# Gate, up and the experts' first weights as seven block products in place of eight, in a gated MLP with a mixture of experts

## The chip, the core and the metric

The kernel runs on one NeuronCore of a Trainium2 chip. The metric is device time in microseconds (us): the median of several executions. One execution was also recorded by the hardware profiler. The engines are TensorE (PE, with its weight loads as PEld), VectorE (DVE), ScalarE (ACT), GpSimd (POOL), and SyncE (SP), which here only issues transfers. Each engine takes its instructions in one fixed order, which the compiler has chosen from the program's text and the dependences.

## What is computed

1024 tokens of 512 features are normalised (layer norm). From the result `xn` two things are made and multiplied, and the input is added:

```python
s = silu(xn @ w_gate.T)                   # 1024 x 1376
k = 1376 // 2
# per token: the k entries of smallest |s| become 0
s = s.at[rows, top_k(-abs(s), k)].set(0.0)
s = (s * (xn @ w_up.T)) @ w_down.T        # 1024 x 512

scores = softmax(xn @ router_w + router_b) + router_bias   # 16 experts in 4 groups
# the 2 best groups, and in them the 2 best experts of each token
y = sum over experts e: gate[e] * ((silu(xn @ w1[e] + b1[e]) * (xn @ w2[e] + b2[e])) @ w3[e] + b3[e])
z = the same form with the shared weights (inner size 256, as two experts of 128)
out = x + s * silu(y + z)
```

Everything is fp32. w1 and w2 of an expert are 512 x 128, w3 is 128 x 512.

## The kernel before

`quick_path` does all the work in the case at hand; a second path, `general_path`, would run after it only if a flag said that the quick search had failed, or that more than two routed experts were used. The tokens are eight tiles of 128. An fp32 matmul takes two passes of TensorE.

**Inputs.** SP loads tile 0 of x, the first 512 columns of the gate weights, tiles 1 to 3, the rest of the gate weights, and then the router's weights, which stand as 16 more columns behind the gate's 1376 (`GW` = 1392). `stats` (L565) and `normalise` (L585) make mean and deviation on DVE in a chain of small operations, subtract and scale; PE transposes the tile into `xnT`, 4 chunks of 128 features by 1024 tokens, and ACT copies it out of PSUM.

**Gate.** `gate(t, k)` (L601 to L617) multiplies a tile by one of the three column ranges `COLS` (512, 512, 352; the last with the router's 16 columns: 368). Four chunks accumulate in one of eight PSUM banks, ACT applies silu, `S[t]` takes the result. `absolute` (L619) makes magnitudes `A[t]` and their sum on ACT, into buffers with the tag `row`.

**Search.** `Search` (L632) finds for each token the threshold below which exactly half of its magnitudes lie. It begins from the mean; each of four `step`s counts the entries under the candidate and corrects it. A count is one pass over 1376 entries, on DVE (L648) or on ACT (L653); the first search, tiles 0 to 3, puts two of four counts on DVE, the second, tiles 4 to 7, none. `last` (L668) does three passes per tile on DVE (count, keep those below, eight greatest), `thresholds` picks the exact value in eight small operations, and `mask` (L706) zeroes the small entries.

**Experts.** `choose` finds each token's experts; `fetch` makes row numbers from it and gathers the weights of the two experts in use by indirect transfers on POOL's queue. `expert` (L856) multiplies 512 tokens at a time by w1 and w2, silu on ACT, product on DVE.

**Up and down.** `up(t)` (L842) has the form of `gate`; DVE multiplies its result into `S[t]` (L853). `finish(t)` (L875) does the second expert products (L881), sums them with the gates on DVE, applies silu, transposes `S[t]` on PE (L905, ACT copies to `sT`), multiplies by `w_down` (L921, 11 chunks), and multiplies and adds on DVE and POOL (L924, L926). Then SP stores the tile.

The program's order is: gate of tiles 0 to 3, the first search beside gate of tiles 4 to 7, shared experts, last of the first search, up of tiles 0 to 3, the second search, up of tiles 4 to 7, routed experts, and the eight `finish`. `wd_sb` uses the gate weights' memory and is loaded when the gate is done.

Of the kernel before, what the change touches and what calls it, by code (L numbers as in the profile page):

```python
# [19 lines left out]
P = 128  # L20
H = 512
# [22 lines left out]
ROW_BUFS = 5  # L44
SLOTS = 2
GW = I + E

# [434 lines left out]
def quick_path(  # L482
# [16 lines left out]
    NT = N_TOK // P  # L499

# [6 lines left out]
    dram = ctx.enter_context(tc.tile_pool(name="dram", bufs=1, space=DRAM))  # L507
# [6 lines left out]
    def load_x(t, again=""):  # L514
        xt = work.tile([P, H], F32, tag="x", name=f"x{again}{t}", bufs=4)
        nc.sync.dma_start(xt, x[ts(t, P), :])
        return xt

    wg_sb = big.tile([P, IC * H], F32, tag="wgd", name="wg_sb")[:, : HC * GW].rearrange(
        "p (c n) -> p c n", c=HC  # L520
    )
    wg_v = wg.rearrange("(c p) n -> p c n", p=P)

    X = {0: load_x(0)}
    lo, n = COLS[0]
    for c in range(HC):
        nc.sync.dma_start(wg_sb[:, c, :n], wg[ts(c, P), :n])  # L527
    for t in range(1, 4):
        X[t] = load_x(t)
    for lo, n in COLS[1:]:  # L530
        nc.sync.dma_start(wg_sb[:, :, lo : lo + n], wg_v[:, :, lo : lo + n])
    nc.sync.dma_start(wg_sb[:, :, I:], rw)
# [10 lines left out]
    b3s_sb = const.tile([P, H], F32, tag="b3s", name="b3s_sb")  # L543
    nc.gpsimd.dma_start(b3s_sb, b3[E].partition_broadcast(P))
# [16 lines left out]
    xnT = big.tile([P, HC, N_TOK], F32, tag="xnT", name="xnT")  # L561
    mv = const.tile([P, NT, 2], F32, tag="mv", name="mv")
    rstd = const.tile([P, NT], F32, tag="rstd", name="rstd")

    def stats(t0, n):  # L565
        for t in range(t0, t0 + n):
            st = small.tile([P, 6], F32, tag="st", name=f"st{t}")
            nc.vector.bn_stats(st, X[t])  # L568
            nc.vector.bn_aggr(mv[:, t, :], st)


        r = rstd[:, t0 : t0 + n]
        ve = small.tile([P, n], F32, tag="ve", name=f"ve{t0}")
        nc.vector.tensor_single_scalar(ve, mv[:, t0 : t0 + n, 1], EPS, ALU.add)
# [3 lines left out]
        q = small.tile([P, n], F32, tag="q", name=f"q{t0}")  # L578
# [6 lines left out]
    def normalise(t0, n):  # L585
        for t in range(t0, t0 + n):
            xn = work.tile([P, H], F32, tag="xn", name=f"xn{t}")
            nc.vector.tensor_scalar(
                xn, X[t], mv[:, t, 0:1], rstd[:, t : t + 1], ALU.subtract, ALU.mult
            )  # L590
            pt = psum(f"pt{t}")
            for c in range(HC):
                nc.tensor.transpose(pt[:, ts(c, P)], xn[:, ts(c, P)], ident)
            nc.scalar.copy(xnT[:, :, ts(t, P)], pt.rearrange("p (c n) -> p c n", c=HC))  # L594
# [6 lines left out]
    def gate(t, k):  # L601
        lo, n = COLS[k]
        w = n + E if k == 2 else n
        if k == 0:
            S[t] = rows.tile([P, I], F32, tag=f"s{t}", name=f"s{t}")
        pz = psum(f"pz{t}_{lo}")
        for c in range(HC):
            nc.tensor.matmul(  # L608
                pz[:, :w],
                xnT[:, c, ts(t, P)],  # L610
                wg_sb[:, c, lo : lo + w],
                start=(c == 0),
                stop=(c == HC - 1),
            )
        nc.scalar.activation(S[t][:, lo : lo + n], pz[:, :n], AF.Silu)  # L615
        if k == 2:
            nc.vector.tensor_tensor(lg[:, t, :], pz[:, n : n + E], rb_sb, ALU.add)  # L617

    def absolute(t):  # L619
        A[t] = row(f"a{t}")[:, :I]  # L620
        nc.scalar.activation(A[t], S[t], AF.Abs, accum_out=asum[:, t : t + 1])  # L621
# [10 lines left out]
    class Search:  # L632
        def __init__(self, t0, n, on_dve):
            self.t0, self.n, self.on_dve = t0, n, on_dve
# [6 lines left out]
        def step(self, k):  # L641
            t0, n = self.t0, self.n
            d = small.tile([P, n], F32, tag="d", name=f"d{t0}_{k}")
            for i in range(n):
                c, cnt = self.c[:, i : i + 1], d[:, i : i + 1]
                if i < self.on_dve:
                    junk = work.tile([P, I], BF16, tag="junk_d", name=f"jd{t0}_{k}_{i}", bufs=1)
                    nc.vector.tensor_scalar(  # L648
                        junk, A[t0 + i], c, None, ALU.is_lt, ALU.add, accum_out=cnt
                    )  # L650
                else:
                    junk = work.tile([P, I], BF16, tag="junk_a", name=f"ja{t0}_{k}_{i}", bufs=1)
                    nc.scalar.activation(  # L653
                        junk, A[t0 + i], AF.Sign, bias=c, scale=-1.0, accum_out=cnt
# [13 lines left out]
        def last(self, i0, i1):  # L668
            t0, n = self.t0, self.n
            if i0 == 0:  # L670
                self.cnt = small.tile([P, n], F32, tag="cnt", name=f"cnt{t0}")
                self.v = small.tile([P, n, 8], F32, tag="v", name=f"v{t0}")
            for i in range(i0, i1):
                w = rows.tile([P, I], F32, tag="w", name=f"w{t0 + i}")
                nc.vector.tensor_scalar(
                    w, A[t0 + i], self.c[:, i : i + 1], None, ALU.is_lt, ALU.add,
                    accum_out=self.cnt[:, i : i + 1],
                )
                nc.vector.scalar_tensor_tensor(  # L679
                    w, A[t0 + i], self.c[:, i : i + 1], A[t0 + i], ALU.is_lt, ALU.mult  # L680
                )
                nc.vector.max(self.v[:, i, :], w)

        def thresholds(self):
# [19 lines left out]
            nc.vector.tensor_scalar(bad[:, t0 : t0 + n], over, -1.0, 1.0, ALU.mult, ALU.add)  # L704
# [385 lines left out]
```

## Time and profile before

| What | Value |
|---|---|
| Median of three runs | 346.39 us (345.88 to 347.0) |
| The profiled execution's own time | 346.43 us |
| Its span, first to last instruction | 344.6 us |
| PE busy | 327.0 us, 95% of the span |
| PEld busy | 161.2 us, 47% |
| DVE busy | 158.7 us, 46% |
| ACT busy | 90.7 us, 26% |
| POOL busy | 22.3 us, 6% |
| Mean granted clock of PE | 0.993 |
| Moved by DMA | 18.99 MB |

Busy times are the union of an engine's instructions; an engine that is busy for a small share of the span may still be full in one stage. The profile gives instructions in groups: the line of the program, the engine, the operation, what is written from what is read, partitions x elements, how many, their busy time and the mean ns of one, and the engine's idle time just before them with what ended it. The chain of waits goes back from the last instruction, at each step to what released it. Its costliest lines are L921 (22% of the span), L846 (21%) and L608 (21%).

### The profile page before, as it was taken

The page shows a single profiled execution, that of the slowest core. Times are in us where ns is not written, and L with a number is a line of the kernel's source. Part 1 is how long each engine was busy: PE and PEld are TensorE (multiplying, and loading weights), DVE is VectorE, ACT ScalarE, POOL GpSimd, SP SyncE. Part 2 cuts the span into 40 slices and gives each one's busy share as a digit, 9 for nine tenths or more (in the row PEclk, how much of TensorE's full clock was granted, in tenths as well). Part 3 has the DMA queues.
Part 4 walks back from the last instruction along what each step waited for, and adds up shares of the span by engine and source line. Part 5 has one row for each costly group of instructions (what it writes and reads, how often), then busy time and mean ns, then how long its engine had stood idle before and what let it go on. Part 6 is the DMA issues. An engine that isn't in the chain of part 4 may idle for free.

```text
span 344.6 us, 2574 instructions
## 1 busy us (share of the span) xinstructions
PE 327.0 (95%) x898; PEld 161.2 (47%) x898; DVE 158.7 (46%) x353; ACT 90.7 (26%) x149; POOL 22.3 (6%) x30
## 2 busy tenths in 40 slices
PE   1899999999999999999999999999999999999991
PEld 0344465444444444445454444454454544544480
DVE  4752005999978323987983300123150431504300
ACT  1322169861169787000000010020120201202010
POOL 4000000000000000460000000001010010110100
PEclk9999999999999999999999999999999999999997
DMA  6989002000090000160000000000010110000000
GB/s 193 324 307 355 2 0 61 0 1 2 2 320 6 0 0 2 39 187 18 0 0 2 0 0 1 0 2 34 27 61 0 63 50 11 30 0 30 33 19 22
DMA packets 10165, 18.99 MB, mean 55 GB/s; under 512 B 1360, under 2 KB 2688, under 8 KB 10144
## 3 DMA queue, kind: packets, MB, share of 16 engines
q1 hardware_dynamic: 9328, 16.35, 13.6%
q0 software_dynamic: 816, 2.39, 2.6%
q8 instruction: 9, 0.15, 0.2%
q14 instruction: 12, 0.10, 0.1%
HBM read 16.65 MB, written 2.10 MB: 54 GB/s over the span
## 4 chain that ended last, share of the span: by engine, by line
PE 92%; DMA 2%; DVE 2%; ACT 1%; SPq 1%; issue 0%
PE po L921 22%; PE pu L846 21%; PE pz L608 21%; PE pys L881 4%; PE pbr L863 4%; PE par L863 4%; PE pbs L863 4%; PE pas L863 4%; PE pyr L881 4%; PE ps L905 3%; DMA x<-in_x_dram 2%; SPq L527 0%; ACT xnT L594 0%; ACT a L621 0%; DVE st L568 0%; ACT s L615 0%
## 5 line engine op out<-in xcount | busy, mean ns | idle before, releaser
L608 PE MATMUL pz<-wg_sb,xnT 128*128 128x512 f32 (+1 forms) x192 | 78.7, 571 | 1.7 <-ACT xnT L594 1.6
L921 PE MATMUL po<-wd_sb,sT 128*128 128x512 f32 (+3 forms) x198 | 77.7, 549 | 0.0
L846 PE MATMUL pu<-wu_sb,xnT 128*128 128x512 f32 (+1 forms) x192 | 74.2, 548 | 0.0
L608 PEld LDWEIGHTS pz<-wg_sb,xnT 128*128 128x128 f32 x192 | 37.2, 196 | 41.4 <-issue 31.3
L846 PEld LDWEIGHTS pu<-wu_sb,xnT 128*128 128x128 f32 x192 | 36.4, 190 | 37.4 <-issue 29.7
L921 PEld LDWEIGHTS po<-wd_sb,sT 128*128 128x128 f32 (+1 forms) x198 | 37.0, 190 | 36.1 <-issue 33.5
L924 DVE TENSOR_TENSOR g<-po,g 128x512 f32<-128x512 f32 (+1 forms) x9 | 5.7, 632 | 70.5 <-PE po L921 70.5
L653 ACT ACTIVATE ja<-a,c 128x1376 bf16<-128x1376 f32 x24 | 34.6, 1440 | 6.3 <-DVE c L666 5.9
L907 ACT COPY sT<-ps 128x512 f32<-128x512 f32 (+1 forms) x24 | 11.5, 516 | 92.9 <-PE ps L905 92.9
L615 ACT ACTIVATE s<-pz 128x512 f32<-128x512 f32 (+1 forms) x24 | 13.1, 547 | 44.1 <-PE pz L608 44.1
L870 ACT ACTIVATE hr<-par,bs 128x512 f32<-128x512 f32 x4 | 2.8, 688 | 80.9 <-PE par L863 80.9
L853 DVE TENSOR_TENSOR s<-s,pu 128x512 f32<-128x512 f32 (+1 forms) x24 | 14.6, 626 | 10.9 <-PE pu L846 10.9
L926 POOL TENSOR_TENSOR g<-g,xr 128x512 f32<-128x512 f32 x7 | 8.8, 1263 | 162.3 <-DVE g L924 162.3
L881 PE MATMUL pys<-w3shared,hs 128*128 128x512 f32 x32 | 15.1, 595 | 0.0
L881 PE MATMUL pyr<-w3slot,hr 128*128 128x512 f32 x32 | 15.0, 592 | 0.0
L863 PE MATMUL pas<-xnT,w12shared 128*128 128x512 f32 x32 | 14.4, 592 | 0.0
L863 PE MATMUL pbs<-xnT,w12shared 128*128 128x512 f32 x32 | 14.4, 592 | 0.0
L863 PE MATMUL par<-xnT,w12slot 128*128 128x512 f32 x32 | 14.4, 592 | 0.0
L863 PE MATMUL pbr<-xnT,w12slot 128*128 128x512 f32 x32 | 14.4, 592 | 0.0
L871 DVE SCALAR_TENSOR_TENSOR hr<-pbr,bs,hr 128x512 f32<-128x512 f32 x4 | 3.0, 750 | 23.1 <-PE pbr L863 23.1
L648 DVE TENSOR_SCALAR_CACHE_REDUCE jd<-a,c 128x1376 bf16<-128x1376 f32 x8 | 13.2, 1646 | 0.2
L679 DVE SCALAR_TENSOR_TENSOR w<-a,c 128x1376 f32<-128x1376 f32 x8 | 13.2, 1648 | 0.1
(124 smaller groups left out, 235.9 us busy)
## 6 DMA issues: line engine op xcount, KB each, us to landing
wd_sb<-in_wd_dram SPq DMA_DIRECT2D x1, 2560.0 KB, 10.5
x<-in_x_dram SPq DMA_DIRECT2D x8, 256.0 KB, 5.7
wu_sb<-in_wu_dram SPq DMA_DIRECT2D x2, 1024.0 KB, 9.7
xr<-in_x_dram SPq DMA_DIRECT2D x8, 256.0 KB, 2.8
out_dram<-g SPq DMA_DIRECT2D x7, 256.0 KB, 2.0
wg_sb<-in_wg_dram SPq DMA_DIRECT2D x4, 256.0 KB, 5.8
wg_sb<-in_wg_dram SPq DMA_DIRECT2D x1, 1024.0 KB, 9.8
w12shared<-in_wexp_dram SPq DMA_DIRECT2D x2, 512.0 KB, 5.5
```

What stands on the lines that cost most here:

```text
L608: nc.tensor.matmul(pz[:, :w], xnT[:, c, ts(t, P)], wg_sb[:, c, lo : lo + w], start=(c == 0), stop=(c == HC - 1),)
L615: nc.scalar.activation(S[t][:, lo : lo + n], pz[:, :n], AF.Silu)
L648: nc.vector.tensor_scalar(junk, A[t0 + i], c, None, ALU.is_lt, ALU.add, accum_out=cnt)
L653: nc.scalar.activation(junk, A[t0 + i], AF.Sign, bias=c, scale=-1.0, accum_out=cnt)
L679: nc.vector.scalar_tensor_tensor(w, A[t0 + i], self.c[:, i : i + 1], A[t0 + i], ALU.is_lt, ALU.mult)
L846: nc.tensor.matmul(pu[:, :n], xnT[:, c, ts(t, P)], wu_sb[:, c, lo : lo + n], start=(c == 0), stop=(c == HC - 1),)
L853: nc.vector.tensor_mul(S[t][:, lo : lo + n], S[t][:, lo : lo + n], pu[:, :n])
L863: nc.tensor.matmul(pk, w[0][:, k * H + c * P : k * H + (c + 1) * P], xnT[:, c, cols], start=(c == 0), stop=(c == HC - 1),)
L881: nc.tensor.matmul(py, h[:, ts(t, P)], w, start=(i == 0), stop=(i == len(which) - 1))
L905: nc.tensor.transpose(pt[:w, ts(c - c0, P)], s[:, c * P : c * P + w], ident)
L907: nc.scalar.copy(sT[:, c0 : c0 + full, :], pt[:, : full * P].rearrange("p (c n) -> p c n", c=full),)
L921: nc.tensor.matmul(po, sT[:w, c, :], wd_sb[:w, c, cols], start=(c == 0), stop=(c == IC - 1))
```

## The change

A product of two matrices cut into 2 x 2 blocks takes eight block products; Strassen's form (here with Winograd's sums) takes seven, and additions of blocks ahead of them and behind. In the changed kernel:

- Two tiles, j and j + 4, make a pair: the first is the upper, the second the lower block row. The 512 features are halved into the block columns. `xs` holds seven blocks: A11, A12, A21, A22 and the sums S1, S2, S4; S3 replaces A21. `sums(j)` makes them with four DVE operations.
- The weights' columns are halved too (gate 2 x 696 with the router's columns, up 2 x 688, an expert's w1 and w2). `weight_sums` makes T1, T2, T4, and replaces B12 by T3, with four operations, on DVE (`V`) or POOL (`G`) as listed.
- `Unit` is a set of seven products, in four PSUM banks X, Y, W, Z, for a pair and a quarter of the columns (344 or 348 wide), or for an expert and 512 tokens. Part `a` makes X and Y, `b` makes W and Z, `c` accumulates three more products on X, W and Z. U = X + Y and V = W + Z are formed in between by an ACT copy and a DVE addition each. `Line.push` interleaves a unit's `a`, the previous unit's `c`, and the unit's `b`.
- Of the gate's four results only the first is silu'd out of PSUM; the other three are sums with U or V that are written to `S` first, and `absolute` applies silu to them in memory. In up the sums go to `tmp`, and POOL multiplies three of the four quarters into `S`.
- There are four searches of two tiles each, with one count on DVE and one on ACT. They are handed to `Line.push` as work to be placed behind a unit's `c`.
- Memory: the gate weights' space later holds the hidden values and the second expert's weights; `wu` and then `wd` share one space, so that `wd` is loaded after up. `row` has four buffers in place of five.
- The order is: gate of the four pairs, the shared experts, the first routed expert, up of pair 0, the second routed expert, up of pairs 1 to 3, and then the eight `finish`, with the expert products of three tiles ahead.

```diff
+    def sums(j):
+        def blk(b):
+            return xs[:, b, :, ts(j, P)]
+        nc.vector.tensor_add(blk(S1), blk(A21), blk(A22))
+        nc.vector.tensor_sub(blk(S3), blk(A11), blk(A21))
+        nc.vector.tensor_sub(blk(S2), blk(S1), blk(A11))
+        nc.vector.tensor_sub(blk(S4), blk(A12), blk(S2))
+    def weight_sums(eng, b11, b21, b12, b22, t1, t2, t4):
+        first = eng[0].tensor_tensor(t1, b12, b11, ALU.subtract)
+        eng[1].tensor_tensor(b12, b22, b12, ALU.subtract)
+        eng[2].tensor_tensor(t2, b22, t1, ALU.subtract)
+        eng[3].tensor_tensor(t4, b21, t2, ALU.subtract)
+        return first
...
+        def a(self):
+            self.X, self.Y = self.acc("x"), self.acc("y")
+            self.mm(self.X, A11, "b11", True, True)
+            self.mm(self.Y, S2, "t2", True, True)
+            self.U = work.tile([P, HALF], F32, tag="U", name=f"U{self.name}")[:, : self.n]
+            nc.scalar.copy(self.U, self.X)
+            self.summed = nc.vector.tensor_tensor(self.U, self.U, self.Y, ALU.add)
+        def b(self):
+            self.W, self.Z = self.acc("w"), self.acc("z")
+            self.mm(self.W, S1, "t1", True, True)
+            self.mm(self.Z, S3, "b12", True, True)
+            self.V = work.tile([P, HALF], F32, tag="V", name=f"V{self.name}")[:, : self.n]
+            nc.scalar.copy(self.V, self.W)
+            nc.vector.tensor_tensor(self.V, self.V, self.Z, ALU.add)
+        def c(self):
+            self.mm(self.X, A12, "b21", False, True)
+            self.mm(self.W, S4, "b22", False, True)
+            self.mm(self.Z, A22, "t4", False, True)
+            self.sink(self)
...
+    def gate_unit(d, j, q):
...
+        def sink(u):
+            l, r = slice(q * n, (q + 1) * n), slice(half + q * n, half + (q + 1) * n)
+            nc.scalar.activation(top[:, l], u.X, AF.Silu)
+            nc.vector.tensor_tensor(top[:, r], u.W, u.U, ALU.add)
+            nc.vector.tensor_tensor(bot[:, l], u.Z, u.U, ALU.add)
+            add = nc.gpsimd if j < NP - 1 else nc.vector
+            add.tensor_tensor(bot[:, r], u.U, u.V, ALU.add)
...
+    def up_unit(d, j, q):
...
+        def sink(u):
+            nc.vector.tensor_mul(top[:, l], top[:, l], u.X)
+            for s, acc, which in ((top[:, r], u.W, "w"), (bot[:, l], u.Z, "z")):
+                m = tmp(u, which)
+                nc.vector.tensor_tensor(m, acc, u.U, ALU.add)
+                nc.gpsimd.tensor_tensor(s, s, m, ALU.mult)
+            nc.gpsimd.tensor_tensor(u.U, u.U, u.V, ALU.add)
+            nc.gpsimd.tensor_tensor(bot[:, r], bot[:, r], u.U, ALU.mult)
...
+    def expert_unit(name, w, b1, b2, h):
...
+        def sink(u):
+            nc.scalar.activation(ht, u.X, AF.Silu, bias=b1)
+            m = tmp(u, "z")
+            nc.vector.tensor_tensor(m, u.Z, u.U, ALU.add)
+            nc.scalar.activation(hb, m, AF.Silu, bias=b1)
+            m = tmp(u, "w")
+            nc.vector.tensor_tensor(m, u.W, u.U, ALU.add)
+            nc.vector.scalar_tensor_tensor(ht, m, b2, ht, ALU.add, ALU.mult)
+            nc.vector.tensor_tensor(u.U, u.U, u.V, ALU.add)
+            nc.vector.scalar_tensor_tensor(hb, u.U, b2, hb, ALU.add, ALU.mult)
...
+        g = work.tile([P, H], F32, tag=("U", "V", "tmp")[t % 3], name=f"g{t}")
...
+    for j in range(NP):
...
+        if j == 0:
+            sum_quarter(dg, 0, GQ, [V, V, V, G])
+        sums(j)
+        if j == 0:
+            sum_quarter(dg, GQ, GQ, [V, G, V, G])
...
+        def begin(j=j):
+            if j:
+                search[j - 1].step(2)
+                search[j - 1].step(3)
+                select(j - 1)
+            absolute(j)
+            search[j] = Search(j)
+        line.push(gate_unit(dg, j, 0), steps(j - 1, (0, 1)) if j else None)
+        line.push(gate_unit(dg, j, 1), begin)
...
+    line.push(shared(0, w12_first))
+    nc.sync.dma_start(w12_second[:, : 2 * H], wexp[E + 1, :, : 2 * H])
+    chosen = choose()
+    line.push(shared(1, w12_second), steps(NP - 1, (0, 1, 2, 3)))
+    routed, mix, fetch_weights = fetch(*chosen, [w12_third, w12_second], slot_w3)
+    du = blocks(wu_sb, I // 2, "u")
+    for q in range(2):
+        sum_quarter(du, q * UQ, UQ, [G, G, G, G])
+    fetch_weights(0)
+    line.push(routed_unit(0), lambda: select(NP - 1))
+    fetch_weights(1)
+    for j in range(NP):
+        for q in range(2):
+            line.push(up_unit(du, j, q))
+            if (j, q) == (0, 1):
+                line.push(routed_unit(1))
+    line.flush()
...
+    wd_sb = big.tile([P, IC * H], F32, tag="wB", name="wd_sb").rearrange("p (c n) -> p c n", c=IC)
...
+    ahead = 3
+    gt = {t: experts_out(t, ex, mix) for t in range(ahead)}
     for t in range(NT):
-        if t < 4:
-            qb.mask(t)
-        finish(t, ex, mix)
+        finish(t, gt.pop(t))
+        if t + ahead < NT:
+            gt[t + ahead] = experts_out(t + ahead, ex, mix)
```

`experts_out(t)` is the first half of what was `finish(t)`: the second expert products, their sum with the gates, and silu. `select(j)` is `last`, `thresholds` and the two masks of pair j.

## The prediction

> **What bounds it now.** I read the chain of waits first, then the same chain in order of time, then busy times by stage, then rows by shape. The chain is almost all TensorE:
>
> ```profile
> PE 92%; DMA 2%; DVE 2%; ACT 1%; SPq 1%; issue 0%
> ```
>
> In order of time (start, length, what) from 22.56 us to 337.15 there is no gap that matters in it; three pieces price a matmul pass:
>
> ```profile
> 55.82 37.63 PE pz L608 x96
> ...
> 93.45 3.43 PE pas L863 x8
> ...
> 120.92 9.23 PE pu L846 x24
> ```
>
> Eight passes of 512 columns take 3.43, one 0.429. A tile of up (16 passes of 512, 8 of 352) takes 9.23, so a 352-wide pass takes (9.23 - 6.86)/8 = 0.296. A tile of gate takes 37.63/4 = 9.41. An fp32 matmul is two passes.
>
> Busy times by stage (stretch, length, then PE, PEld, DVE, ACT, POOL):
>
> ```profile
> 0.00:22.56 22.56, 12.92 (x32) 6.01 (x32) 13.04 (x63) 5.46 (x8) 3.58 (x15) 1.00 0.80 260
> 22.56:55.80 33.24, 32.72 (x96) 16.89 (x96) 6.44 (x28) 12.15 (x21) 0.00 (x0) 1.00 0.37 132
> 55.80:93.45 37.65, 37.63 (x97) 18.51 (x98) 35.03 (x60) 20.30 (x32) 0.00 (x0) 1.00 0.04 13
> 93.45:120.90 27.45, 27.45 (x66) 12.14 (x65) 18.10 (x55) 21.09 (x29) 0.00 (x0) 1.00 0.30 103
> 120.90:195.00 74.10, 74.10 (x196) 36.71 (x195) 47.85 (x95) 12.87 (x19) 9.84 (x8) 1.00 0.10 29
> 195.00:222.50 27.50, 27.50 (x67) 11.90 (x65) 4.42 (x5) 2.75 (x4) 0.00 (x0) 1.00 0.00 0
> 222.50:337.20 114.70, 114.64 (x352) 59.01 (x350) 33.03 (x48) 16.12 (x40) 8.84 (x7) 1.00 0.08 27
> ```
>
> The reader is to see the DVE column: to 222.5 it sums to 124.9, over half of the time, and in the search it is 93% busy already. The last stage, which the change hardly touches, is where DVE is free.
>
> **PE: what is removed.** Each unit of a pair of tiles is 7 products x 2 chunks x 2 passes = 28 passes. At 348 columns (0.292, in proportion to 352) gate is 8 units x 28 x 0.292 = 65.4 in place of 8 x 9.41 = 75.3; up, at 344 (0.289), 64.7 in place of 73.8; the experts 4 x 28 x 0.429 = 48.0 in place of 16 x 3.43 = 54.9. Removed: 9.9 + 9.1 + 6.9 = 25.9 us. The weight load stays hidden: its rows are 190 ns, under a pass of 289.
>
> **Start.** At 22.56 PE had done two gate groups and four tiles' transposes, 6.9 + 2.1 = 9.0 us, as if it had begun at 13.6 without a gap. After, the second product needs tile 4, both sums and the weight sums. Tile 4 is the fourth transfer, behind 0.97 MB (tile 1 was behind 1.31 MB and came at 9.9): about 8. Then a serial chain as tile 0 shows it, 3.24 to 9.5, gives 14.3, less the sums; four sums in series, 4 x 0.46, overlap in part: 15.5. By then 2.2 us of PE work is done and, the first gate group having taken 6.61 where 3.43 is usual, some 2 are lost to a slow start: as if from 15.3, 1.7 later. Bounds -1 and +6 (tile 4 as late as tile 1, loads of short rows).
>
> PE alone: 346.43 - 25.9 + 1.7 = **322.2**.
>
> **DVE: what is added.** Rows by shape:
>
> ```profile
> L679 DVE SCALAR_TENSOR_TENSOR w<-a,c 128x1376 f32<-128x1376 f32 x8 | 13.2, 1648 | 0.1
> L648 DVE TENSOR_SCALAR_CACHE_REDUCE jd<-a,c 128x1376 bf16<-128x1376 f32 x8 | 13.2, 1646 | 0.2
> L853 DVE TENSOR_TENSOR s<-s,pu 128x512 f32<-128x512 f32 x16 | 10.7, 682 | 7.5 <-PE pu L846 7.5
> L926 POOL TENSOR_TENSOR g<-g,xr 128x512 f32<-128x512 f32 x7 | 8.8, 1263 | 162.3 <-DVE g L924 162.3
> L853 DVE TENSOR_TENSOR s<-s,pu 128x352 f32<-128x352 f32 x8 | 4.1, 514 | 3.4 <-PE pu L846 3.4
> L924 DVE TENSOR_TENSOR g<-po,g 128x256 f32<-128x256 f32 x2 | 0.8, 424 | 9.3 <-PE po L921 9.3
> ```
>
> - `sums`: 16 x 0.424 = 6.8. `weight_sums` on DVE: 5 of 696 elements (0.69 + 184 x 1.05 ns = 0.885) = 4.4, and 16 of 256 for the experts = 6.8.
> - Gate units, which cost DVE nothing before: 34 x 0.51 = 17.4. Expert units: 5 more each of 512, 20 x 0.69 = 13.8. Up: 40 x 0.51 less 14.8 now = 5.6.
> - Search: one count of two on DVE in place of two of eight, 8 more x 1.73 (with the accumulator's read) = 13.8. ACT loses as many. Steps' small operations, 96 for 44, 52 x 0.165 = 8.6; starts and `thresholds` for four searches in place of two, 3.6.
> - `stats`: one more chain of 15 x 0.155 = 2.3.
>
> Sum 83.1: DVE needs 124.9 + 83.1 = **208 us** before the down stage can run freely, PE only 183. Bounds: 202 operations are added; of independent operations the next begins before the last ends, of dependent ones 0.04 later:
>
> ```profile
> 149.33 0.75 DVE L890 SCALAR_TENSOR_TENSOR g<-b3r,gs,b3s_sb 128x512 f32<-128x512 f32 x1
> 150.00 1.65 DVE L679 SCALAR_TENSOR_TENSOR w<-a,c 128x1376 f32<-128x1376 f32 x1
> 151.56 0.68 DVE L853 TENSOR_TENSOR s<-s,pu 128x512 f32<-128x512 f32 x1
> 152.16 1.59 DVE L682 MAX8 v<-w 128x8 f32<-128x1376 f32 x1
> ```
>
> 0.67 apart for a row of 0.75: -0.08 x 202 = -16 at best, +0.04 x 202 = +8 at worst. So 192 to 216. I take 208, as both kinds mix. These lines also show that the compiler's order puts an eviction or a late addition between two operations of a search. An eviction so waits about one 1.65 us operation, not a whole `select`, and PE, which comes back to a unit's bank 4.7 us later, is not held unit by unit. It is held by the total.
>
> **Other engines.** ACT gains 40 copies to U and V (0.45 to 0.6) and loses eight counts: under 100 us of 220, hidden. POOL has 11 weight sums of about 1.7 (1.26 x 696/512), 6 additions and 32 operations of 0.86 in up, about 3.5 us per 8.1 us unit: hidden unless a mask is late, since it works in order and its product waits for the masked row. SP: tiles 3 and 7 are queued behind the late loads (3.3 MB, some 10 us at the 300 to 355 GB/s of the page's second to fourth slices), due by 60: hidden. `wd` now takes the place of `wu`, so its 10.5 us load can start only after up's last matmul; the three tiles of expert products put ahead (3 x 3.43 = 10.3) are its cover. If they wait for DVE (their `g` lies in U, V and tmp, which the last pair holds until its masks), up to 10.5 us come out.
>
> **The sum.** DVE begins at 3.24. Until the first magnitudes are there (about 41) its work is fed by transfers and PE; I give it 6 idle (2 to 12). The last masks end at D = 3.24 + 6 + 208 = 217. Then 2 us of multiplications and the down stage of 114.65, less two tiles of expert products done ahead (6.9), and the 7.4 us from its last matmul to the end of the span: 217 + 2 + 107.8 + 7.4 = 334.2, and 1.83 outside the span: 336. PE alone says 322. Between them PE is free to do tile 0's transposes and down product (10.8) if banks allow; I count 4 us of it. Forecast **332 us**, against 346.43 profiled and 346.39 median.
>
> The Trainium skill speaks against the change here. SBUF — State Buffer, section "Who interferes with whom", says that a DVE instruction with two SBUF inputs and a GpSimd instruction that reads SBUF exclude each other for the whole instruction. Nothing before shows it: POOL's seven additions ran beside DVE operations on PSUM. By that rule some 75 two-input operations, with POOL busy 30% of the time and half an operation of 0.9 to wait, add about 10 us (an estimate): 342.
>
> **Rivals.**
> 1. *PE stays the bound*, 322 (319 to 325). For: evictions slip between search operations, and up's last pair needs only the pair before it masked. Against: 208 us of DVE against 183 of PE in the same stages.
> 2. *DVE's queue decides: slower.* The time is D + 119, so it passes 346.4 at D = 227.5, 10.5 us above mine. With dependent pitch (216), 12 idle, and DVE held in order by three transfers as it now is 3.3 us before L890 for b3r (10), D is 241 and the time 360; with half of these excesses 348. For: no slack, and the fetched weights' sums put DMA waits into DVE's queue. Against: the dense pitch above.
> 3. *The routed experts come late.* `choose` and `fetch` are some 50 dependent operations, 12 us now; if each waits for a search operation, 80 more. PE has shared experts and two pairs of up until about 141, so every microsecond beyond counts from there; slower than before if the routed products start after 165. Against: the steps' own short chains leave slots every 0.2 us. About 350.
> 4. *It does less than it says*: only the 10.5 us of `wd` lie bare on rival 1's path, 333; this falls in my own band.
>
> **Chances.** Forecast (325 to 343) 0.50; rival 1 0.14; rivals 2 and 3 0.22 and 0.07; 0.07 between 343 and 347.4. A measurement can tell 0.3%, 1 us, from no change: faster 0.67, same 0.04, slower 0.29. Range 321 to 354: rival 1's upper half to most of rival 2. The likeliest case's own range is 325 to 343.
>
> **What would show it.** The passes of gate at about 0.292 and 224 records of each of gate and up; DVE over 90% busy from about 45 until the last `select`; PE's idle lying late in up or just ahead of the down stage, named as waiting for DVE; the wd load issued after the last up matmul. Wrong if PE is at 99% from 30 us on (rival 1), if DVE is idle while PE waits (a wait I don't see, rivals 2 and 3), or if DVE or POOL rows are longer than these.

## The result and the profile after

The changed kernel takes 383.76 us (median of 4 executions, 381.38 to 385.98) beside 346.17 for the kernel before (345.88 to 347.0): a ratio of 1.108, with a 95% interval of 1.1011 to 1.115. It is slower by 37.6 us; the forecast was 332 us, and the time lies above the whole range. The profiled execution is the longest of the four, 385.98 us; its span is 383.7. Now and then an execution falls into a slower state: ratios are of the fast ones alone, while the medians of e4 and e6 below include one slow execution each.

The first view is the chain of waits of the changed kernel, its shares by engine:

```profile
PE 56%; DVE 34%; issue 3%; DMA 3%; ACT 1%; POOL 1%; SPq 0%; DVEq 0%; POOLq 0%
```

Before, PE held 92% of it. Now a third of the chain is work on DVE. Where that lies is read from the span in 40 slices of 9.6 us (busy tenths of PE and of DVE, and the granted PE clock):

```profile
PE   0399987969298750029999999999999999999993
DVE  4888799999999999999732433239821420320010
PEclk9999999999789985559999999999999999999998
```

DVE is full from the sixth slice to the nineteenth, and in the same stretch PE sinks, to nothing in slices 16 and 17. From slice 19 on PE is full to the end, while DVE falls to a third of its time. So PE's loss is all in the first 170 us. The windows (stretch, length, then PE, PEld, DVE, ACT, POOL busy, clock, DMA share, GB/s) give its size:

```profile
0.00:17.75 17.75, 1.99 (x8) 1.62 (x9) 11.44 (x40) 1.87 (x2) 4.83 (x16) 1.00 0.74 236
...
53.00:93.10 40.10, 33.24 (x122) 21.12 (x120) 39.56 (x98) 23.39 (x36) 5.52 (x4) 1.00 0.06 14
93.10:142.60 49.50, 35.91 (x77) 15.08 (x75) 48.85 (x103) 21.52 (x33) 11.97 (x8) 0.90 0.03 11
142.60:169.82 27.22, 0.80 (x4) 0.50 (x3) 26.96 (x93) 5.33 (x7) 5.02 (x6) 0.56 0.18 55
169.82:262.10 92.28, 91.22 (x282) 53.53 (x282) 45.51 (x81) 12.07 (x24) 29.24 (x31) 0.98 0.05 13
```

PE idles 6.9 and 13.6 us in the later gate pairs and the shared experts (53 to 142.6), and 26.4 us ahead of the first routed expert. In up (169.82 to 262.1) it idles 1.1 us, with DVE busy for 45.5 of 92.3. PE's order of time (start, length, what, idle before and what ended it) has the two longest waits of 93 to 142.6, and then what PE waited for from there:

```profile
103.93 2.69 PE L718 MATMUL pzg<-t4g,xs 128*128 128x348 f32 x4 [7.47 <-DVE Vg L654]
...
138.96 3.65 PE L1012 MATMUL pzes<-xs,moe 128*128 128x512 f32 x4 [2.38 <-DVE Ves L654]
160.39 0.79 PE L911 MATMUL pc<-bothe,ones 128*128 128x128 f32 x2 [17.78 <-DVE bothe L873]
169.82 3.58 PE L1012 MATMUL pxer<-xs,w_third 128*128 128x512 f32 x4 [8.63 <-DMA w_third<-in_wexp_dram,wrow]
```

`bothe` is the router's last choice; `w_third` are the weights fetched by it. DVE's order of time shows why they are late, and one thing more:

```profile
92.79 1.04 DVE L800 TENSOR_TENSOR m<-d 128x2 f32<-128x2 f32 x1
93.87 1.57 DVE L801 SCALAR_TENSOR_TENSOR m<-m,slope 128x2 f32<-128x2 f32 x1
95.48 1.56 DVE L802 SCALAR_TENSOR_TENSOR d<-d,m 128x2 f32<-128x2 f32 x1
97.07 1.55 DVE L803 TENSOR_TENSOR c<-c,d 128x2 f32<-128x2 f32 x1
...
103.37 0.50 DVE L654 TENSOR_TENSOR Vg<-Vg,pzg 128x348 f32<-128x348 f32 x1
...
122.49 0.27 DVE L878 TENSOR_REDUCE mx<-lg 128x8 f32<-128x128 f32 x1
...
144.81 0.17 DVE L827 TENSOR_TENSOR hit<-iota,cnt 128x16 f32<-128x16 f32 x1
144.90 0.18 DVE L861 TENSOR_TENSOR prg<-v2g,tmg 128x32 f32<-128x32 f32 x1
145.00 1.59 DVE L818 MAX8 v<-w 128x8 f32<-128x1376 f32 x1
146.50 0.17 DVE L862 TENSOR_TENSOR prg<-prg,order 128x32 f32<-128x32 f32 x1
...
160.05 0.29 DVE L873 TENSOR_TENSOR bothe<-ohe,ohe 128x128 f32<-128x128 f32 x1
```

From the router's first operation (L878) to its last (L873) it is 37.6 us. In the kernel before the same two are 11.9 us apart:

```profile
100.51 0.29 DVE L746 TENSOR_REDUCE mx<-lg 128x8 f32<-128x128 f32 x1
...
112.45 0.29 DVE L741 TENSOR_TENSOR bothe<-ohe,ohe 128x128 f32<-128x128 f32 x1
```

Lines 144.81 to 146.50 show how: between two operations of the choice (L861 and L862, 0.2 us each) stands one of a search (L818, 1.6 us), of pair 2, which up needs last but one. In the program's text pair 2's last two steps and its selection stand ahead of `choose`, as `begin` of pair 3 hands them in; pair 3's counts, of which two stand among the choice too (at 153.09 and 156.55), the text has behind `fetch`, and it was the compiler that put them there. At 92.79 the other thing: four operations on two elements of each partition, 0.16 us elsewhere, take 1.04 to 1.57 us while GpSimd adds up's weights (from 92.17, 1.65 us a sum). The eviction Vg stands behind them and some operations of the searches; it comes at 103.37, and PE waits 7.5 us for it. The same is seen at the start, beside one of GpSimd's sums of gate weights:

```profile
13.78 1.65 POOL L626 TENSOR_TENSOR t4g<-wg_sb,t2g 128x696 f32<-128x696 f32 x1 [9.68 <-DVE q L594]
...
13.98 1.45 DVE L596 TENSOR_TENSOR rstd<-rstd,q 128x1 f32<-128x1 f32 x1
```

The long rows that answer to those before are of the size foreseen; there are twice as many counts (L785), and as many products (L815):

```profile
L785 DVE TENSOR_SCALAR_CACHE_REDUCE jd<-a,c 128x1376 f32<-128x1376 f32 x16 | 26.2, 1638 | 0.1
...
L815 DVE SCALAR_TENSOR_TENSOR w<-a,c 128x1376 f32<-128x1376 f32 x8 | 13.1, 1643 | 0.0
```

### The profile page after: what moved, and what is told of

Same layout as the page of the kernel before. It is cut to its first block, busy times and chain, and to the rows that moved or that the text cites. A ratio compares the mean times of both kernels' runs of the same rounds, so it can differ in the third digit from the quotient of the medians.

```text
span 383.7 us, 3011 instructions
## 1 busy us (share of the span) xinstructions
PE 312.5 (81%) x946; PEld 172.3 (45%) x946; DVE 235.1 (61%) x563; ACT 95.6 (25%) x165; POOL 76.1 (20%) x78
## 4 chain that ended last, share of the span: by engine, by line
PE 56%; DVE 34%; issue 3%; DMA 3%; ACT 1%; POOL 1%; SPq 0%; DVEq 0%; POOLq 0%
PE po L1081 20%; DVE jd L785 6%; PE pzu L718 5%; PE pxu L718 5%; PE pwu L718 4%; PE pys L1037 4%; PE pyr L1037 3%; DVE w L815 2%; DVE s L845 2%; PE pyu L718 2%; DVE v L818 2%; PE ps L1065 2%; PE pwer L1012 2%; PE pzer L1012 2%; DMA x<-in_x_dram 2%
## 5 line engine op out<-in xcount | busy, mean ns | idle before, releaser
L1086 POOL TENSOR_TENSOR g<-g,xr 128x512 f32<-128x512 f32 x7 | 8.9, 1267 | 92.3 <-DVE g L1084 79.2
L785 DVE TENSOR_SCALAR_CACHE_REDUCE jd<-a,c 128x1376 f32<-128x1376 f32 x16 | 26.2, 1638 | 0.1
L718 PE MATMUL pxg<-wg_sb,xs 128*128 128x348 f32 x64 | 23.7, 502 | 2.0 <-ACT xs L607 1.5
L718 PE MATMUL pxu<-wu_sb,xs 128*128 128x344 f32 x64 | 21.1, 452 | 0.0
L718 PE MATMUL pzg<-t4g,xs 128*128 128x348 f32 x32 | 12.1, 506 | 9.7 <-DVE Vg L654 9.7
L718 PEld LDWEIGHTS pxg<-wg_sb,xs 128*128 128x128 f32 x64 | 12.7, 207 | 9.8 <-ACT xs L607 2.4
L718 PEld LDWEIGHTS pxu<-wu_sb,xs 128*128 128x128 f32 x64 | 12.2, 190 | 7.2 <-issue 1.4
L911 PE MATMUL pc<-bothe,ones 128*128 128x128 f32 x2 | 0.8, 501 | 17.8 <-DVE bothe L873 17.8
L1037 PE MATMUL pys<-w3shared,moe 128*128 128x512 f32 x32 | 15.1, 595 | 0.0
L1037 PE MATMUL pyr<-w3slot,moe 128*128 128x512 f32 x32 | 15.0, 592 | 0.0
L718 PE MATMUL pyg<-t2g,xs 128*128 128x348 f32 x32 | 12.2, 507 | 3.3 <-DVE xs L618 3.3
L811 DVE TENSOR_SCALAR_CACHE_REDUCE w<-a,c 128x1376 f32<-128x1376 f32 x8 | 13.1, 1641 | 0.1
L815 DVE SCALAR_TENSOR_TENSOR w<-a,c 128x1376 f32<-128x1376 f32 x8 | 13.1, 1643 | 0.0
L845 DVE SCALAR_TENSOR_TENSOR s<-a,thr,s 128x1376 f32<-128x1376 f32 x8 | 13.1, 1640 | 0.0
```

Of the source, the lines that this page charges most:

```text
L718: nc.tensor.matmul(acc, xs[:, blk, c, ts(j, P)], d[key][:, c, lo : lo + acc.shape[1]], start=first and c == 0, stop=last and c == 1, skip_ ...
L785: nc.vector.tensor_scalar(junk, self.A[i], c, None, ALU.is_lt, ALU.add, accum_out=cnt)
L811: nc.vector.tensor_scalar(w, self.A[i], self.c[:, i : i + 1], None, ALU.is_lt, ALU.add, accum_out=self.cnt[:, i : i + 1],)
L815: nc.vector.scalar_tensor_tensor(w, self.A[i], self.c[:, i : i + 1], self.A[i], ALU.is_lt, ALU.mult)
L845: nc.vector.scalar_tensor_tensor(s, self.A[i], self.thr[:, i : i + 1], s, ALU.is_gt, ALU.mult)
L1037: nc.tensor.matmul(py, h[:, ts(t, P)], w, start=(i == 0), stop=(i == len(which) - 1))
```

## The experiments

Two theories stood against each other. *Order*: DVE's work is not too much, but it stands in the wrong order: searches that nobody needs yet lie between the router's operations and ahead of PE's evictions, and PE's own order has the routed experts ahead of up. Two smaller causes go with it, the *lock* seen at 92.79 (operations of DVE held while GpSimd adds) and the *late start*. *Total*, the prediction's own idea: DVE's load has to be done, whatever the order. Every run was timed in 3 rounds together with the kernel before (346.8 to 347.2 us), those from e8 on in 5; the changed kernel stands beside them with its 383.76. An edit is against the changed kernel where nothing else is said, and `...` marks what is left out.

**e1: up's weight sums later.** In the changed kernel:

```diff
-    for q in range(2):
-        sum_quarter(du, q * UQ, UQ, [G, G, G, G])
...
-    fetch_weights(0)
+    asked = fetch_weights(0)
+    for q in range(2):
+        sum_quarter(du, q * UQ, UQ, [G, G, G, G], after=asked)
```

> The eight weight sums of up on GpSimd (688 wide, 1.65 us each) are moved behind the first routed expert's indirect loads; nothing is left out. Theory of the lock (GpSimd's sum makes two-element operations of VectorE last 1.04 to 1.59 us at 92 to 101 us of the changed kernel): those five operations are back at 0.15 to 0.2 us, the eviction Vg behind them is done near 97 instead of 103.4, and TensorE's gap of 7.5 us there is gone; the end moves by about -7 (376 us), less what the same lock now costs the first routed expert's weight sums (0 to +6). Rival (the lock is only an effect beside a queue that is late anyway): the small operations are short again but the time stays at 381 to 386.

390.85 us (389.22 to 392.1), 1.1267 of before (1.1204 to 1.133). The first part came true: the logits' last addition is at 113.62 in place of 121.75, and the first routed product at 160.72 in place of 169.82. Then more than the gain was lost, at the place to which the sums were moved. DVE in order of time:

```profile
160.04 12.72 DVE L821 SCALAR_TENSOR_TENSOR w<-a,c 128x1376 f32<-128x1376 f32 x1
172.69 0.41 DVE L623 TENSOR_TENSOR w_third<-w_third 128x256 f32<-128x256 f32 x1
```

And GpSimd in the same time:

```profile
160.14 3.23 POOL L623 TENSOR_TENSOR t1u<-wu_sb 128x688 f32<-128x688 f32 x2
...
169.69 1.62 POOL L631 TENSOR_TENSOR t2u<-wu_sb,t1u 128x688 f32<-128x688 f32 x1
```

One operation of a search, 1.65 us elsewhere, lasted 12.72: it ended 1.45 us after GpSimd's seventh sum (169.69 + 1.62 = 171.31). The first routed expert's weight sums stood behind it, and PE waited 11.4 us for them. In the profiled executions this adds up: the span is 3.2 us longer (386.9 for 383.7) though the product came 9.1 earlier, and of these 12.3 us the wait makes 10.9 (11.44 for 0.59) and the slower product behind it 1.4. So the lock is real and sized on both sides: 8 us at the old place, 11 at the new. The step "less what the same lock now costs" was put at 0 to 6 and was too small.

**e2: the last searches behind the router.**

```diff
-            if j:
-                search[j - 1].step(2)
+            logits(j)
+            if j == NP - 1:
+                chosen.extend(choose())
+            elif j:
+                search[j - 1].step(2)
...
+    def last_searches():
+        search[NP - 2].after = search[NP - 1].after = indices
+        steps(NP - 2, (2, 3))()
+        select(NP - 2)
+        steps(NP - 1, (0, 1, 2, 3))()
...
+        select(NP - 1)
...
+    line.push(routed_unit(0), last_searches)
```

> The same work in another order on VectorE: the last two search steps and the selection of pair 2 and the whole search of pair 3 are put behind the router's chain (choose, and the indices of the indirect loads); the third weights of the routed experts are asked for after pair 2's selection, because their tile comes free there. Theory of the order: the chain from the logits (121 us) to the last choice takes about 18 us (12.4 as in the kernel before, and some five evictions between) in place of 38, the indirect loads are issued near 143 instead of 163, the first routed product starts near 150 instead of 169.8, and the end is near 365 us (360 to 370). Rival of the total (VectorE's 208 us have to be done whatever their order): VectorE does the same work, so the end stays at 380 to 386, with TensorE waiting later, in up.

369.39 us (368.19 to 371.06), 1.0626 (1.0567 to 1.0684): 14.4 us less than the changed kernel, inside the expected band. DVE is busy for 238.2 us, 3 more than before the edit: the same work, and the end is earlier. That decides against the total, which had the end at 380 to 386. PE at the same two places:

```profile
139.76 0.80 PE L923 MATMUL pc<-bothe,ones 128*128 128x128 f32 x2 [4.88 <-DVE bothe L885]
148.67 3.73 PE L1026 MATMUL pxer<-xs,w_third 128*128 128x512 f32 x4 [8.12 <-DMA w_third<-in_wexp_dram,wrow]
```

The choice took 17.5 us (121.89 to 139.41) and the routed product came at 148.67, as foreseen (18 and 150). The 4.4 us missing to 365 were given back in up: PE waits there 1.1, 2.1 and 3.0 us for evictions that now stand among the searches.

**e3: PE's order alone.**

```diff
+    for q in range(2):
+        line.push(up_unit(du, 0, q))
     routed, mix, fetch_weights = fetch(*chosen, [w12_third, w12_second], slot_w3)
...
-    for j in range(NP):
+    for j in range(1, NP):
```

> Only TensorE's order is changed: the two units of up of pair 0 (16.2 us) stand before the first routed expert, and the choice's count of tokens (the ones matmul) stands behind them. Theory of the order: TensorE's hole from 142.6 to 169.8 us is filled with these 16.2 us, the routed products start up to 6 us later than 169.8 because the units' evictions come between the router's operations, and the end is at 367 to 376 us. Rival of the total: VectorE has the same work to do, so TensorE waits as long elsewhere: 380 to 386.

377.8 us (376.66 to 380.33), 1.0903 (1.0832 to 1.0974): 6.0 us less. The routed product came at 176.69, 0.9 later than the latest that was foreseen, since the router's operations now had these units' evictions among them too (43 us for the choice). 16.2 us of PE work were moved into the hole and 6.9 of them lost to the later product. The time lies 1.8 us above the expected band and 2.2 below the total's; e2 is the clearer of the two.

**e4: the start alone.**

```diff
-    X = {0: load_x(0)}
+    X = {0: load_x(0), NP: load_x(NP)}
...
-            stats(0, 0, 1)
+            stats(0, 0, 2)
             normalise(0, 0)
-            stats(0, 1, 1)
             normalise(0, 1)
...
-            sum_quarter(dg, 0, GQ, [V, V, V, G])
+            sum_quarter(dg, 0, GQ, [V, V, V, V])
...
-            sum_quarter(dg, GQ, GQ, [V, G, V, G])
+            sum_quarter(dg, GQ, GQ, [V, V, V, V])
```

> Only the start is changed: tile 4 is loaded right behind tile 0, both are normalised in one chain of 15 small operations instead of two, and the weight sums of the first pair are all on VectorE (none on GpSimd). Theory of the late start: the second transposes come near 10 us instead of 16.9, TensorE is as if it had begun near 13 to 15 instead of 21.5, and the end is 5 to 9 us earlier, 375 to 379, as all that follows moves with it. Rival (the router's chain alone sets the end and VectorE's queue before it is full anyway): the start is earlier by as much, but the logits of pair 3 still come near 121 us and the time stays at 381 to 386.

383.0 us (380.38 to 386.74), 1.1013 (1.0916 to 1.1109). Not told apart from the changed kernel by its time; the trace shows 4 us: the logits' last addition at 116.64 in place of 121.75, the routed product at 165.64 in place of 169.82. The second transposes came at 9 to 11 as foreseen, but the second product waited 3.83 us for the block sums, which stood behind the weight sums, and those for weights that landed at 12.55. So less could be had at the start than was expected, and this run does not show whether it reaches the end.

**e7: up's weight sums on DVE.**

```diff
-        sum_quarter(du, q * UQ, UQ, [G, G, G, G])
+        sum_quarter(du, q * UQ, UQ, [V, V, V, V])
```

> From the changed kernel one thing alone: the eight weight sums of up are on VectorE (0.89 us each) and no longer on GpSimd (1.65 each). Theory of the lock (while GpSimd adds from two rows of SBUF, VectorE's operations on two rows of SBUF stand still, so that GpSimd's 13.2 us cost VectorE more than doing them): no operation of VectorE lasts over 2 us, the first routed product starts at 161 to 168 us in place of 169.8, and the end is 2 to 8 us earlier than the changed kernel's 383.8, 376 to 382. Rival of the total (VectorE's load decides): 7.1 us more on VectorE, so 391.

383.91 us (382.83 to 384.97), 1.1045 (1.0971 to 1.1119). Neither theory's number. Without the lock the logits are complete at 113.13, 8.6 us earlier; the eight sums of 0.89 us then stand among the router's operations (41 us for the choice), and the routed product comes at 166.42. So the lock cost about what doing the sums on DVE costs: GpSimd's help was worth nothing here, and moving the sums alone is worth nothing either.

**e5: all together**, with both counts of the last two searches on ScalarE.

```diff
+ON_DVE = (1, 1, 0, 0)
...
+        if j + 1 < NP:
+            prepare(j + 1)
...
+    line.push(up_unit(du, 0, 0))
+    routed, mix, fetch_weights, indices = fetch(*chosen, [w12_third, w12_second])
...
+    line.push(up_unit(du, 0, 1), last_searches)
+    line.push(routed_unit(0))
```

> All that the first four runs point to, together; nothing of the computation is left out. Tile 4 loaded behind tile 0, one chain of statistics for both, and each pair normalised and summed while the units of the pair before run; all weight sums of gate and up on VectorE (8 x 0.89 us more there, GpSimd's 13.2 us of sums gone); the searches of pairs 2 and 3 behind the router's chain and both their counts on ScalarE (8 x 1.73 us less on VectorE); the units of up of pair 0 ahead of the first routed expert, with the count of tokens between them. Theory of order, lock and start: from the 369 of the run with the late searches go 5 (start), 12 (TensorE's two holes ahead of the routed products, 4.9 and 8.1), 7 (lock at 92 to 104) and 4 (TensorE's waits in up): 341 us, 336 to 352. Rival of the total: that run had VectorE busy without a gap from about 56 to 222; of this load 13.8 goes and 7.1 comes, so the end is at 369 - 7 - 5 = 357 or later.

353.25 us (349.97 to 355.08), 1.0182 (1.0111 to 1.0254): 1.2 us above the theory's band and 4 below the earliest of the total. PE's waits named the rest: 3.71 us for pair 1's normalised tiles, 3.29 for the block sums, 3.91 for the fetched weights.

**e6: pair 1's search late too**, with the routed experts side by side ahead of up's pair 1. Against e5:

```diff
-ON_DVE = (1, 1, 0, 0)
+ON_DVE = (1, 0, 0, 0)
...
+        steps(1, (0, 1, 2, 3))()
+        select(1)
+        absolute(NP - 1)
...
     fetch_weights(1)
+    line.push(routed_unit(1))
     for j in range(1, NP):
```

> As the run before, and the search of pair 1 too is put behind the router (its four steps with both counts on ScalarE, its selection on VectorE after the indices), with the second routed expert ahead of up's pair 1 to give it time; nothing is left out. Theory: in the stage of gate VectorE has some 25 us less to do and TensorE's waits there for evictions and sums (5.9 + 4.9 in the run with the late searches) go, while up, where VectorE is half idle, takes the work: 8 us less than the run beside it, 333. Rival of the total: the work is only moved, up's evictions then wait behind three searches, and the time is that of the run beside it or 5 to 15 us more.

356.0 us (352.13 to 357.62), 1.0199 (1.0087 to 1.0312). Its executions overlap with those of e5, and 333 is excluded: this is what the rival had foreseen. The first half of the theory came true, the routed product at 140.24 in place of 146.78; then up paid: waits of 2.84 us for the second expert's weight sums and 4.26 for an eviction. Work moved out of one full stage had filled the next, so DVE's load in a stage counts as well as its order.

**e8 and e9: the three waits mended, and the last counts on ScalarE.** e8 against e5:

```diff
-        if j + 1 < NP:
+        if 0 < j < NP - 1:
             prepare(j + 1)
         line.push(gate_unit(dg, j, 1), begin)
+        if j == 0:
+            prepare(1)
...
+    line.push(up_unit(du, 1, 0))
     line.push(routed_unit(0))
```

In e8 `sums` also stands ahead of the first pair's weight sums. e9 adds, in `last` of the searches of pairs 2 and 3:

```diff
-                w, self.A[i], self.c[:, i : i + 1], None, ALU.is_lt, ALU.add,
-                accum_out=self.cnt[:, i : i + 1],
+                nc.scalar.activation(
+                    junk, self.A[i], AF.Sign, bias=self.c[:, i : i + 1], scale=-1.0,
+                    accum_out=self.cnt[:, i : i + 1],
+                )
```

> The run with all changes together, mended at the three places where its TensorE still waited: pair 1 is normalised after both units of pair 0 (it waited 3.71 us at its transposes, whose tiles are the last to land), the first pair's block sums stand ahead of its weight sums (a wait of 3.29), and one more unit of up stands ahead of the first routed expert (a wait of 3.91). Theory of order: 353 - 3.7 - 1.4 - 3.9 = 344 us, 340 to 350, and so even with the kernel before or faster. Rival (what is left is no longer a matter of these places; a wait removed comes back at the next eviction that VectorE is late with): 350 or more, slower than the kernel before.

> As the run beside it, and the last count of the searches of pairs 2 and 3 is on ScalarE too (4 x 1.73 us less on VectorE, 4 x 1.44 more on ScalarE). If VectorE's load in up still holds TensorE there, this is 2 to 5 us less than the run beside it; if not, the same within 1 us.

e8: 347.97 us (345.96 to 349.58), 1.0004 (0.9972 to 1.0036); e9: 346.4 us (344.55 to 348.08), 0.9959 (0.9924 to 0.9994). e8 is even with the kernel before, 4 us above the expected number and inside its band. e9 is 1.6 less, between its two cases: the executions of the two overlap, and this is not settled.

**e10 and e11: sums and up earlier.** e10 puts `prepare(j + 1)` ahead of both units of pair j for pairs 1 and 2, and the order of PE is up's pair 0, the count of tokens, pair 1, both routed experts, pairs 2 and 3; e11 has the second expert behind pair 2. e11's order of PE, against e9:

```diff
     line.push(up_unit(du, 0, 0))
+    line.push(up_unit(du, 0, 1))
     routed, mix, fetch_weights, indices = fetch(*chosen, [w12_third, w12_second])
...
-    line.push(up_unit(du, 0, 1), last_searches)
-    line.push(up_unit(du, 1, 0))
+    line.push(up_unit(du, 1, 0), last_searches)
+    line.push(up_unit(du, 1, 1))
     line.push(routed_unit(0))
...
+            if (j, q) == (2, 1):
+                line.push(routed_unit(1))
```

> From the run with the last counts on ScalarE (346.4 us) two orders are changed: pairs 2 and 3 are normalised and summed a unit earlier (ahead of both units of the pair before), and both units of up's pair 0 stand ahead of the count of tokens, both of pair 1 behind it, then the two routed experts, then pairs 2 and 3. Theory of order: TensorE's wait of 4.10 us for the sums of pair 3, and those of 2.97 (count of tokens), 1.20 (weight sums of the first routed expert) and 3.06 (an eviction behind a selection) go, 11 us in all, of which some 4 come back at the next late eviction: 339 us, 336 to 343, faster than the kernel before. Rival (each wait removed is paid again by the one after it, as VectorE has no free time between 40 and 160 us): 345 to 348.

> As the run beside it, with the second routed expert behind pair 2 of up instead of ahead of it. If VectorE needs the second expert's 13.7 us of TensorE time to finish the selection of pair 2, TensorE waits for it at pair 2 and this run is 2 to 6 us later; if not, the two agree within 1 us.

e10: 343.44 us (341.88 to 344.35), 0.9893 (0.9857 to 0.9929); e11: **340.99 us** (340.63 to 341.95), 0.983 (0.9797 to 0.9863). Both are faster than either kernel of the case, than the one before by 1.1 and 1.7%; none of their executions reaches one of that kernel's. In e10 the four named waits are gone, and about 8 of 11 us came back at late evictions, twice what was allowed; the time is 0.4 us above the expected band. For e11 the expectation was on the wrong side: side by side the two experts crowd DVE (e10 has a wait of 2.95 us at 186.79 for the second one's eviction), and apart they don't. Of e11's page, busy times, then PE's two longest waits for other engines behind the start:

```profile
PE 309.8 (91%) x946; PEld 172.9 (51%) x946; DVE 220.3 (65%) x531; ACT 112.1 (33%) x189; POOL 56.5 (17%) x67
```

```profile
63.63 2.69 PE L725 MATMUL pwg<-wg_sb,xs 128*128 128x348 f32 x4 [3.84 <-ACT Vg L660]
...
159.72 2.66 PE L725 MATMUL pzu<-t4u,xs 128*128 128x344 f32 x4 [4.35 <-DVE Vu L661]
```

DVE is busy for 220.3 us here and 235.1 in the changed kernel, 6% less; the time is 43 us, 11%, less.

## Why the prediction was wrong

The sum, from the prediction's own "PE alone": 322.2, and on it 6.2 for the start, 20.5 for waits in gate and the shared experts, 26.4 for the hole ahead of the routed expert, are 375.3. The last 10.7 to the profiled 385.98 are slower matmuls behind the gaps and 1.1 us of waits in up: PE is busy for 312.5 us, where 327.0 - 25.9 = 301.1 was due, and some 1.6 of these 11.4 lie in the start already.

- *What PE saves* was right: a group of four passes follows the one before at 1.17 us in gate and 1.16 in up, so 0.292 and 0.289 a pass. The 25.9 us are in the kernel; in e11 5.8 of them reach the time.
- *The start* failed in size: "as if from 15.3", with a bound of +6, and it was about 21.5 (by 53.0 PE had done 25 groups of 1.17 us and four tiles' transposes, some 31.5 us of work). Tile 4 landed at 8.67 (about 8 foreseen). The step that failed is "a serial chain as tile 0 shows it": DVE put the first weight sums between that chain's operations, one operation of it lasted 1.45 us beside a sum on GpSimd, the normalised tile was begun at 16.25, 7.6 us behind the chain's first operation, where tile 0 of the kernel before took 3.8 (3.24 to 7.05), and the block sums ran from 18.61 to 23.45, one of them 1.87 us long beside another sum on GpSimd, for 0.41.
- *What DVE gains in work* was right in size: 76.4 us over the span, for 83.1; to the end of up 200.9, for 208, inside 192 to 216. Some 9 of these are not work but the lock: e7 does up's sums on DVE as well (8 x 0.89 = 7.1), and DVE is busy for 233.2 us there, 1.9 less.
- *"It is held by the total"* is the step that failed first. The last masks ended at 185, not at 217, and D + 119 would have made 304. The end of the span came 199 us after them. Not the load held PE, but what of it came first. e2 shows it: the same load, 14.4 us.
- *"An eviction so waits about one 1.65 us operation ... and PE ... is not held unit by unit"* was wrong too. The row of the products Z of gate has 9.7 us of waits for Vg, 7.5 of them at 103.93, behind the operations that GpSimd held. From 53 to 142.6 PE's waits add up to 20.5 us: 12.1 for V's addition on DVE, most of the rest for block sums and for ACT's copies.
- *Rival 3* was what happened, and it was given 0.07 and 350 us. Its threshold was passed (165; the product came at 169.8), but is not confirmed: in e2 the product came at 148.67, and the time was still 23 us above the kernel before. Its price was too low by the step "PE has shared experts and two pairs of up until about 141": in the program's order the first routed expert stands ahead of up, so PE had nothing to do from 142.6. The diff shows this; I read the units as if PE could choose. PE was late before that, too: by the prediction's own terms the shared experts end near 109 (15.3, 65.4 for gate, 4.2 for transposes, 24.0), and they ended at 142.6. e3 sizes the order: 6 us when the two units of pair 0 are put ahead.
- *Against rival 3* I held "the steps' own short chains leave slots every 0.2 us". They do, and in these slots stood searches: the choice took 37.6 us.
- *GpSimd's sums, "hidden unless a mask is late"*, were not. Nobody waited for them; they stopped DVE. The Trainium skill's rule (SBUF — State Buffer, "Who interferes with whom") was weighed and left out of the sum, for want of a row. The runs agree with it: operations with two inputs in SBUF stood still for the whole of GpSimd's (1.57 us for 0.16), while the search's counts, one input, ran at their usual 1.64. An operation with one input on two elements was held too (L774 at 100.23, 1.59 us), so the rule as the prediction tells it does not cover every row. The estimate of 10 us from it, made for another place (up), is near the 8 us on the logits.
- *The rest held*: the wd load was issued at 260.3, behind the last of up's matmuls that read `wu` (258.87 to 260.19; the four after it read T4), and was covered; SP stayed hidden, and ACT all but for 4.3 us of PE's waits for its copies before 142.6; GpSimd's operations in up took 0.91 to 0.97 us, for 0.86.

What stays open: how much of the slower matmuls is due to which gap, and where e7 lost its gain behind 160 us. Of the three causes only the order moved the end by itself (14.4 us in e2, 6.0 in e3); for the start (e4) and the lock (e7) that was not seen. From e5 on order, start, sums and counts change together, with less work on DVE, so how the 43 us from the changed kernel to e11 share out is not shown.

## What to carry to other kernels

When a change loads a second engine that all stages share, a balance of totals is not enough: write down in which order that engine's queue serves its customers, and when the first engine's *next* instruction in program order has its last input; here the change cost 37.6 us in one order and 14.4 us less with the same DVE work in another, and with all the mends, and 6% less work on DVE, it made the kernel 1.7% faster. A chain of short dependent operations that a transfer waits for should stand ahead of long operations with a later due time, with an explicit dependence if the compiler fills its gaps. And work given to GpSimd was no relief for VectorE where both read two rows of SBUF (383.76 us with up's sums there, 383.91 without).

## What the runs showed of the hardware

- GpSimd's additions stop VectorE's two-input operations on SBUF for their whole length, even those on two elements (1.04 to 1.57 us for 0.16), and one long operation was held through seven additions in a row, 12.72 us for 1.65 (e1). In e7, with none of up's sums on GpSimd, no two-element operation from 85 to 130 us lasts over 0.18. The small operations each got through at the end of one addition; why the long one did not is open.
- A gap of PE is paid twice. Behind the 17.8 and 8.6 us of waiting at 142.6 to 169.8 the first product took 3.58 us, where the same shape takes 1.88 elsewhere, and the granted clock in that stretch was 0.56; but a wait of 4.35 us is enough in e11 for a product of 2.66 in place of 1.32, and one of 2.38 us (138.96) for a product of 3.65 in place of 1.88. The Trainium skill (TensorE: Matmul & The Clock Gate, Part 1) has the clock halved after about 3.4 us without work and restored after as long a time of work. The rows agree in part: the slow groups last 3.6 us at 169.82 and 5 us from 103.93 on, and waits of 0.47 us (260.66) and 0.91 (83.64) leave 1.42 and 1.44 us behind them. But a wait of less than 3.4 us was enough at 138.96, and in e10 a wait of 2.95 us at 186.79 was followed by 3.45 us for 1.88; here the measured rows decide.
